# Layer 3 of a four-layer kernel: one pass over x3 in place of two

## Chip, cores and metric

The kernel runs on one core of a Trainium2 chip. The metric is the device time in microseconds (us) from start to end of one execution; three timed runs of the kernel before gave 3595.99 to 3599.18 us, median 3596.93 us. The profile is of one further execution.

A core has engines that run their own instruction streams in order and wait for each other through semaphores: PE (matrix products; PEld is its weight load), DVE (vector), ACT (activation functions), POOL (general), SP (here it only issues DMAs). DMAs move data between the memory of the chip (DRAM) and the 128 partitions of on-chip memory. PE writes its results to PSUM, a small memory from which DVE and ACT read.

## The reference, cut to what matters

The input is an image x of 256 x 256 positions with 128 channels. Four layers follow, each of the form x = x + layer(groupnorm(x)). The change concerns layer 3:

```python
    def _L3_conv_ref(x, w1, b1, w2, b2):
        H, W = (x.shape[1], x.shape[2])
        relu = jax.nn.relu
        def c1(t):
            return lax.conv_general_dilated(t, w1, (1, 1), 'SAME', dimension_numbers=DN) + b1
        w2c = w2[0, 4]
        def c2(t):
            return jnp.einsum('bhwc,cd->bhwd', t, w2c) + b2
        t = relu(c1(x))
        y = jnp.concatenate([x[:, :1], x[:, 1:] + t[:, :-1]], axis=1)
        u = relu(c1(y))
        z_main = u + jnp.roll(y, 1, axis=1)
        z = jnp.concatenate([z_main[:, :H - 2], u[:, H - 1:H] + y[:, H - 2:H - 1], y[:, H - 1:H]], axis=1)
        v = relu(c2(z))
        p = jnp.concatenate([z[:, :, :1], z[:, :, 1:] + v[:, :, :-1]], axis=2)
        r = relu(c2(p))
        q_main = r + jnp.roll(p, 1, axis=2)
        q = jnp.concatenate([q_main[:, :, :W - 2], r[:, :, W - 1:W] + p[:, :, W - 2:W - 1], p[:, :, W - 1:W]], axis=2)
        return q
```

`c1` is a convolution with nine taps along a row (w1 has the shape 1 x 9 x 128 x 1): it turns 128 channels into one, so t and u are single-channel images of 256 x 256. `c2` is a 128 x 128 product for each position. Since y is x plus t of the row above, and c1 is linear, c1(y) is c1(x) plus the nine taps of t of the row above, weighted with the sums of w1 over the channels. So the nine tap images of x are all that t and u need from x. z is x one row further up, plus a single-channel image e, which is made of u and of t two rows above.

## The kernel before

Layers 0 to 2 come first and leave their result in DRAM as `x3T` (128 channels x 65536 positions). Layer 3 then has three stages.

**p8** (L1116 to L1127), over 32 groups `s` of 2048 positions (eight rows): SP loads 1 MB of x3T into `p8_x` (L1119); four matmuls with `w1f`, the nine taps scaled by the groupnorm's factor, each write their 32 rows of one PSUM tile (L1122, `p_s` in the profile, which leaves out a stage's number in a name); ACT adds `s0` and writes `p_st` (L1126); POOL's queue stores it to the DRAM tensor `sD` (L147).

**img** (L1130 to L1189) makes e for the whole image at once: it loads all nine tap images into `St`, adds them with shifts along the row on DVE (L1153 to L1156), gets t on ACT, the nine taps of t by nine products and sums (L1163 to L1165), u, and e. Shifts by rows go from partition to partition, so t, the taps of t, u and e go through the DRAM tensor `imgD`: a store (`store`, L1136), then loads with the row shift in the address (`load_down`, L1141 and L1142; L1179 to L1187). e ends in `er` (L1206), one DMA for each of four positions groups.

**p9** (from L1199) is a second pass over x3 in 32 steps of eight rows (R = 8). Its order is written out by hand (`tc.manual_schedule()`), so each engine runs its part in the order of the text. In step s:

- `load9(s + 3)` loads nine rows of x3 (the row above is needed for z; L1217);
- ACT writes the first column of `pbs[s]` (L1289), `qs[s]` = x + constant (L1291), and `start_z(s + 1)` writes z without e (L1223);
- `p_half(s, 0)` and `(s, 1)`: two matmuls each into PSUM (`p_pm`, L1238), and a DVE instruction that makes p (L1246);
- `finish_z(s + 1)`: `broadcast_rows` spreads e over the partitions with PE (`p_eb`, L824), DVE adds it to z (L1232);
- `q_half(s - 1, ...)`: again two matmuls and DVE instructions (L1238, L1260, L1263) each, and one column on ACT (L1302);
- `residual(s)` on POOL (L1252 to L1254);
- `emit(s - 2)`: 16 transposes on PE (`p_pt`, L1275), two ACT copies (L1276), and one store of 1 MB by SP (L1277).

PSUM has two buffers for `p_pm` and two (tag "x") that `p_eb` and `p_pt` take in turn: the next user of such a buffer waits until DVE or ACT has read it.

Of the kernel before, what the change touches and what calls it, by code (L numbers as in the profile page):

```python
# [31 lines left out]
def kernel(ctx: ExitStack, tc: tile.TileContext, a: dict, out: bass.AP):  # L32
# [27 lines left out]
    sD = dram.tile([32, T], F32, name="sD")  # L60
    imgD = dram.tile([4, T], F32, name="imgD")
# [81 lines left out]
    b2 = column("L3_conv_b2")  # L143

# [52 lines left out]
    with tc.tile_pool(name="x0", bufs=1) as xres, tc.tile_pool(name="p0", bufs=3) as sb:  # L197
# [18 lines left out]
        with tc.tile_pool(name="f0", bufs=1) as fsb, tc.tile_pool(name="f0ps", bufs=1, space=PSUM) as ps:  # L216
# [29 lines left out]
            pb2 = ps.tile([P, 6], F32, name="f0_pb2")  # L246
# [4 lines left out]
            nc.vector.tensor_tensor(b2w, b2w, pb2, ALU.add)  # L251
            pt_ = ps.tile([P, NH], F32, name="f0_pt")
# [103 lines left out]
    with tc.tile_pool(name="p2c", bufs=1) as cs:  # L356
# [39 lines left out]
        with tc.tile_pool(name="p2", bufs=2) as sb, tc.tile_pool(name="p2e", bufs=6) as eb, tc.tile_pool(  # L396
# [159 lines left out]
            for j in range(2 * NG + 5):  # L556
# [5 lines left out]
                if not 0 <= out[0] < NG:  # L562
                    out = None
                if half == 0 and nxt:
                    tiles(nxt)
# [267 lines left out]
    rs2_pool = ctx.enter_context(tc.tile_pool(name="rs2", bufs=1))  # L833
# [262 lines left out]

    w1f = const.tile([P, 32], F32, name="w1f")
# [3 lines left out]
    kcol = const.tile([P, 3], F32, name="kcol")  # L1101
    with tc.tile_pool(name="f3", bufs=1) as sb, tc.tile_pool(name="f3ps", bufs=1, space=PSUM) as ps:
        pb = ps.tile([P, 1], F32, name="f3_s")
        for q in range(4):
            nc.tensor.matmul(pb[32 * q : 32 * q + 32, :], lhsT=w1f, rhs=m3, start=True, stop=True)
        nc.vector.tensor_scalar(s0, pb, -1.0, None, ALU.mult)
        nc.vector.scalar_tensor_tensor(k0, m3, -1.0, r3, ALU.mult, ALU.mult)

        pw = ps.tile([P, 1], F32, name="f3_w")
        nc.tensor.matmul(pw, lhsT=w2c, rhs=b2, start=True, stop=True)  # L1110
        nc.vector.tensor_scalar(kcol[:, 0:1], b2, -1.0, None, ALU.mult)
        nc.vector.scalar_tensor_tensor(kcol[:, 1:2], pw, -1.0, b2, ALU.mult, ALU.subtract)
        nc.vector.scalar_tensor_tensor(kcol[:, 2:3], b2, 2.0, pw, ALU.mult, ALU.add)

    with tc.tile_pool(name="p8", bufs=4) as sb, tc.tile_pool(name="p8ps", bufs=4, space=PSUM) as ps:
        for s in range(NSC):  # L1116
            ss = slice(s * SC, (s + 1) * SC)
            xt = sb.tile([P, SC], F32, name="p8_x", bufs=6)
            nc.sync.dma_start(xt, x3T[:, ss])  # L1119
            pp = ps.tile([P, CK], F32, name="p8_s")  # L1120
            for c in range(4):
                nc.tensor.matmul(  # L1122
                    pp[32 * c : 32 * c + 32, :], lhsT=w1f, rhs=xt[:, c * CK : (c + 1) * CK], start=True, stop=True
                )
            st = sb.tile([P, CK], F32, name="p8_st", bufs=8)
            nc.scalar.activation(st, pp, AF.Identity, bias=s0)  # L1126
            store_groups(nc.gpsimd, sD, s, st)  # L1127


    with tc.tile_pool(name="img", bufs=1) as sb, tc.tile_pool(name="imgps", bufs=1, space=PSUM) as ps:  # L1130

        def image(k):
            return imgD[k].rearrange("(h w) -> h w", w=N)

        def store(k, t):
            nc.sync.dma_start(image(k).rearrange("(t p) w -> p t w", p=P), t)  # L1136

        def load_down(t, k, n):

            nc.vector.memset(t[0:32, 0, :], 0.0)  # L1140
            nc.sync.dma_start(t[n:P, 0, :], image(k)[0 : P - n, :])  # L1141
            nc.sync.dma_start(t[:, 1, :], image(k)[P - n : N - n, :])  # L1142

        pw = ps.tile([P, TAPS], F32, name="pw")
        nc.tensor.matmul(pw, lhsT=ones, rhs=w1[:, :TAPS], start=True, stop=True)
        wsum = sb.tile([P, TAPS], F32, name="wsum")
        nc.vector.tensor_copy(wsum, pw)
        St = sb.tile([P, TAPS, 2, N], F32, name="St")
        nc.sync.dma_start(
            St.rearrange("p k t w -> p (k t) w"), sD[:TAPS, :].rearrange("k (t p w) -> p (k t) w", p=P, w=N)  # L1150
        )
        acc = sb.tile([P, 2, N], F32, name="acc")
        nc.vector.tensor_copy(acc, St[:, 4, :, :])  # L1153
        shifts = [(k, max(0, 4 - k), min(N, N + 4 - k)) for k in range(TAPS) if k != 4]
        for k, lo, hi in shifts:
            nc.vector.tensor_tensor(  # L1156
                acc[:, :, lo:hi], acc[:, :, lo:hi], St[:, k, :, lo + k - 4 : hi + k - 4], ALU.add
            )
        t_ = sb.tile([P, 2, N], F32, name="t_")
        nc.scalar.activation(t_, acc, AF.Relu, bias=b1)  # L1160
        store(0, t_)
        ct = sb.tile([P, 2, N], F32, name="ct")
        nc.vector.tensor_scalar(ct, t_, wsum[:, 4:5], None, ALU.mult)  # L1163
        for k, lo, hi in shifts:
            nc.vector.scalar_tensor_tensor(  # L1165
                ct[:, :, lo:hi], t_[:, :, lo + k - 4 : hi + k - 4], wsum[:, k : k + 1], ct[:, :, lo:hi],
                ALU.mult, ALU.add,
            )
        store(1, ct)
        cd = sb.tile([P, 2, N], F32, name="cd")  # L1170
        load_down(cd, 1, 1)
        nc.vector.tensor_tensor(acc, acc, cd, ALU.add)
        u_ = sb.tile([P, 2, N], F32, name="u_")
        nc.scalar.activation(u_, acc, AF.Relu, bias=b1)
        store(2, u_)

        eu = sb.tile([P, 2, N], F32, name="eu")
        nc.vector.memset(eu[96:P, 1, :], 0.0)
        nc.sync.dma_start(eu[:, 0, :], image(2)[0:P, :])  # L1179
        nc.sync.dma_start(eu[0 : P - 2, 1, :], image(2)[P : N - 2, :])  # L1180
        nc.sync.dma_start(eu[P - 2 : P - 1, 1, :], image(2)[N - 1 : N, :])
        et = sb.tile([P, 2, N], F32, name="et")
        nc.vector.memset(et[0:32, 0, :], 0.0)
        nc.sync.dma_start(et[0:1, 0, :], image(0)[N - 2 : N - 1, :])
        nc.sync.dma_start(et[2:P, 0, :], image(0)[0 : P - 2, :])
        nc.sync.dma_start(et[0 : P - 2, 1, :], image(0)[P - 2 : N - 4, :])
        nc.sync.dma_start(et[P - 2 : P, 1, :], image(0)[N - 3 : N - 1, :])  # L1187
        nc.vector.tensor_tensor(eu, eu, et, ALU.add)
        store(3, eu)  # L1189
# [8 lines left out]
    H = R // 2  # L1198
    with tc.tile_pool(name="p9", bufs=2) as sb, tc.tile_pool(name="p9psM", bufs=2, space=PSUM) as psM, tc.tile_pool(  # L1199
# [3 lines left out]
        xs, zs, pbs, qs = {}, {}, {}, {}  # L1203
        er = sb.tile([P, CK], F32, name="p9_e", bufs=1)
        for c in range(4):
            nc.sync.dma_start(er[32 * c : 32 * c + 32, :], imgD[3].rearrange("(s c t) -> c s t", c=4, t=CK)[c])  # L1206

        def load9(s):
            if s >= NR:
                return  # L1210
            h0 = s * R
# [7 lines left out]
        def start_z(s):  # L1219
# [4 lines left out]
            if n < R:  # L1224
                nc.scalar.activation(zs[s][:, n:R, :], xs[s][:, n + 1 :, :], AF.Identity, bias=k0, scale=r3)
# [55 lines left out]
        for s in range(3):  # L1281
            load9(s)
# [209 lines left out]
```

## Time and profile before

| what | us |
|---|---|
| median of three runs | 3596.93 |
| the profiled execution | 3590.95 |
| its span (first to last instruction) | 3589.0 |
| layers 0 to 2, and the groupnorm of layer 3, to the first load of x3T at | 3091.9 |
| p8 to its last stores, and St's load begins at | 3205.4 |
| img, to the first p_eb matmul at | 3251.0 |
| p9, to the end | 3589.0 |

The page gives for the whole span PE 87% busy, DVE 64%, ACT 54% and POOL 45%, and a mean granted PE clock of 0.93 of full speed. Those are means over all layers; the table above says where layer 3 lies, and the stage, not the mean, tells what bounds it. A row of the page's groups gives the line, the engine, the operation with output and inputs, how often it ran, its busy time and the mean time of one, and then the idle time before it with what ended that.

In p9's steady part a DMA pair looks like this on SP's queue: the output store is issued in 0.39 us (L1277, at 3377.26), and the load of x3 behind it takes 1.86 us to issue (L1217, at 3377.69), while such a load takes 0.42 us to issue where no store stands ahead (L1214).

### The profile page before, as it was taken

Reading aid. Unit: us, or ns where it says so; the run is one execution under the profiler, and the core shown is the slowest. Engines: PE = TensorE matmul, PEld = TensorE weight load, DVE = VectorE, ACT = ScalarE, POOL = GpSimd, SP = SyncE. Lnnn points to the kernel's source line nnn. Section 1 sums busy time; section 2 is a strip of 40 time slices with the busy share of each in tenths; the row PEclk is TensorE's granted clock in tenths of the full one; section 3 lists DMA queues with packets and bytes.
Section 4 is the critical chain, followed back from the end, with each engine's and each line's share of the span. In section 5 each row is a group of like instructions: output and inputs, shape, how many; then the busy total and the mean of one; then the engine's idle time right before and its main releaser. Section 6 shows DMA issues by size and latency. Waiting matters only on the chain. (4 is left out here: it accounts for less than half of the span.)

```text
span 3589.0 us, 52067 instructions
## 1 busy us (share of the span) xinstructions
PE 3130.1 (87%) x20266; PEld 1649.4 (46%) x20266; DVE 2280.2 (64%) x2522; ACT 1948.9 (54%) x2163; POOL 1631.0 (45%) x852
## 2 busy tenths in 40 slices
PE   4566999999999999955795999998998999636998
PEld 4413555555555555513332444446996333103544
DVE  4625888888888888831695454454555777215776
ACT  3564777777777777632343444443443566414665
POOL 3003777777777777612593000002554444313444
PEclk7887999999999999978897999999998999758999
DMA  9892333333333333278697778667997888675776
GB/s 329 317 344 91 102 119 113 108 114 119 114 110 111 119 117 111 92 296 314 215 329 316 260 259 304 230 245 281 352 351 282 339 336 335 267 284 172 227 226 187
DMA packets 276662, 801.88 MB, mean 223 GB/s; under 512 B 36639, under 2 KB 109612, under 8 KB 221884
## 3 DMA queue, kind: packets, MB, share of 16 engines
q1 hardware_dynamic: 256844, 780.41, 60.9%
q0 software_dynamic: 19568, 18.09, 1.7%
q8 instruction: 162, 2.65, 0.3%
q14 instruction: 88, 0.72, 0.1%
HBM read 504.22 MB, written 294.09 MB: 222 GB/s over the span
## 5 line engine op out<-in xcount | busy, mean ns | idle before, releaser
L468 DVE TENSOR_TENSOR p_e<-p_S,triT 128x1024 f32<-128x1024 f32 x512 | 609.4, 1212 | 144.5 <-PE p_S L458 144.5
L478 POOL TENSOR_TENSOR p_es<-p_e 128x1024 f32<-128x1024 f32 x256 | 603.0, 2366 | 127.5 <-issue 67.5
L476 ACT ACTIVATE p_e<-p_e,mbT 128x1024 f32<-128x1024 f32 x512 | 551.8, 1137 | 63.2 <-DVE p_e L468 61.4
L908 PE MATMUL p_pm<-p_zn,wf 128*128 128x512 f32 x1024 | 443.9, 595 | 15.8 <-DVE p_zn L901 15.8
L443 PE MATMUL p_mm<-p_xn,wf 128*128 128x512 f32 x768 | 409.0, 616 | 8.0 <-POOL p_xn L416 8.0
L416 POOL TENSOR_TENSOR p_xn<-p_xn,p_rs 128x1024 f32<-128x1024 f32 x64 | 153.6, 2400 | 446.4 <-DMA p_rs<-rsD 254.1
L908 PEld LDWEIGHTS p_pm<-p_zn,wf 128*128 128x128 f32 x1024 | 194.8, 191 | 265.1 <-issue 244.5
L458 PE MATMUL p_S<-p_q,p_k 32*128 32x256 f32 x4096 | 295.3, 400 | 5.0 <-DVE p_e L468 5.0
L458 PEld LDWEIGHTS p_S<-p_q,p_k 32*128 32x128 f32 x4096 | 185.8, 184 | 161.5 <-PE p_mm L434 91.7
L1450 PE MATMUL tp_z<-p_B,tp_at 128*128 128x256 f32 x1024 | 250.6, 388 | 0.8 <-DMA p_B<-bD 0.5
L491 PE MATMUL p_o<-p_e,p_v 128*32 128x256 f32 x4096 | 249.2, 384 | 0.0
L1252 POOL TENSOR_TENSOR p_q<-p_q,p_pb 128x2024 f32<-128x2024 f32 x32 | 144.1, 4502 | 220.8 <-DVE p_pb L1246 220.8
L1079 POOL TENSOR_TENSOR p_x<-p_x,p_g 128x2048 f32<-128x2048 f32 x32 | 145.4, 4544 | 182.6 <-DVE p_g L1076 182.6
L1000 POOL TENSOR_TENSOR p_k<-p_k,p_sq 128x512 f32<-128x512 f32 x128 | 162.9, 1273 | 135.8 <-ACT p_sq L998 135.8
L962 POOL DMA_DIRECT2D rs__17975<-rs2D x4 | 2.1, 519 | 466.7 <-DMA rs2D<-p_vc 466.7
L1450 PEld LDWEIGHTS tp_z<-p_B,tp_at 128*128 128x128 f32 x1024 | 185.1, 191 | 23.2 <-DVE tp_at L1441 1.5
L443 PEld LDWEIGHTS p_mm<-p_xn,wf 128*128 128x128 f32 x768 | 126.7, 191 | 113.3 <-issue 90.2
L491 PEld LDWEIGHTS p_o<-p_e,p_v 128*32 128x32 f32 x4096 | 120.5, 110 | 110.0 <-ACT p_g L449 41.5
L999 DVE TENSOR_TENSOR p_k<-tp_z,p_k 128x512 f32<-128x512 f32 x128 | 88.5, 692 | 127.0 <-ACT p_sq L998 127.0
L996 ACT COPY p_K<-tp_z 128x512 f32<-128x512 f32 x128 | 75.1, 586 | 165.4 <-PE tp_z L1450 165.4
L434 PEld LDWEIGHTS p_mm<-wf,p_xn 128*128 128x128 f32 x1024 | 135.5, 193 | 62.9 <-issue 61.9
L939 DVE SCALAR_TENSOR_TENSOR p_b<-p_pm,b2w,p_b 128x1024 f32<-128x1024 f32 x64 | 82.2, 1284 | 125.4 <-PE p_pm L908 111.0
(335 smaller groups left out, 5870.3 us busy)
## 6 DMA issues: line engine op xcount, KB each, us to landing
p_x<-x2T SPq DMA_DIRECT2D x64, 1024.0 KB
p_x<-x1T SPq DMA_DIRECT2D x48, 1024.0 KB
p_x<-x3T SPq DMA_DIRECT2D x31, 1152.0 KB
p_x<-x3T SPq DMA_DIRECT2D x33, 1024.0 KB
p_x<-in_x_dram SPq DMA_DIRECT2D x32, 1024.0 KB
p_x<-xT SPq DMA_DIRECT2D x64, 512.0 KB
p_rs<-rsD SPq DMA_DIRECT2D x64, 512.0 KB
p_rb<-rzD SPq DMA_DIRECT2D x256, 128.0 KB
```

The lines of the kernel that those rows point to most:

```text
L416: nc.gpsimd.tensor_tensor(xn, xn, t["rs"], ALU.mult)
L443: nc.tensor.matmul(pm, lhsT=w, rhs=t["xn"][:, cs_], start=True, stop=True)
L458: nc.tensor.matmul(Ss[h // 2][:, h % 2, u, :], lhsT=t["k"][hp, r * N + u * P : r * N + (u + 1) * P], rhs=t["q"][hp, r * N : (r + 1) * N], ...
L468: nc.vector.tensor_tensor(e[:, :, 2 * p : 2 * p + 2, :].rearrange("p u h n -> p h u n"), Ss[p], triT[:, 2 * p : 2 * p + 2, :, :], ALU.add,)
L476: nc.scalar.activation(e[:, u, :, :], e[:, u, :, :], AF.Exp, bias=mbT[:, u, i : i + 1])
L478: nc.gpsimd.tensor_tensor(es, e[:, 0, :, :], e[:, 1, :, :], ALU.add)
L491: nc.tensor.matmul(t["o"][hp, r % 2, :], lhsT=t["v"][:, r * 2 + u, hp], rhs=e[:, u, h, :], start=(u == 0), stop=(u == 1),)
L908: nc.tensor.matmul(pm[:, c, :], lhsT=wf2[:, i, :], rhs=zns[s][:, k * CK : (k + 1) * CK], start=True, stop=True)
L1000: nc.gpsimd.tensor_tensor(k2, k2, sq, ALU.add)
L1079: nc.gpsimd.tensor_tensor(xs[s], xs[s], gt, ALU.add)
L1252: nc.gpsimd.tensor_tensor(q[:, :, 1 : N - 2], q[:, :, 1 : N - 2], pb[:, :, 0 : N - 3], ALU.add)
L1450: nc.tensor.matmul(pz[:, t, :], lhsT=at[:, u, t * P : (t + 1) * P], rhs=Bc[:, u, :], start=(u == 0), stop=(u == 1))
```

## The change

p8 and img are gone, and p9 does their work in passing. Only one pass over x3 is left.

- `load9` loads eight rows, not nine, into nine buffers (four before), eight steps ahead (three before). The row above comes from the step before's tile, so `start_z` takes two ACT instructions.
- `taps(x, h0, n)` does p8's work for the row group six steps ahead: four matmuls into a PSUM tile `p9_pp` of the two buffers with tag "x" that p_eb and p_pt use too, one ACT instruction to `p9_st`, and four stores by SP (nine tap rows by two image rows each) to `sD`, whose rows are now padded to 264 with zeros or large negative numbers; three small DMAs in layer 0 (at j == 20) fill the padding.
- `load_block(b)` handles 16 image rows (two steps). Partition 16 q + i holds the row i of the block and the columns 32 q onward. The shift of each tap along the row, and the row shift, lie in the DRAM addresses (`sD_shift` has a tap pitch longer by one). Sixteen DMAs of 16 partitions, nine taps and 40 or 32 columns.
- `sum_taps(b)`: one DVE reduction over the nine taps and two short instructions give t. `keep_t(b)` stores t to `tD` and reads it back shifted by a row. `image_u(b)`: one product with nine overlapping windows of t, one reduction and two short instructions. `image_e(b)`: one sum, a store to `eD`, and four small DMAs into one of two `er` tiles.
- In the loop, an even step s sums block b = s//2 + 2 behind p_half and makes u at its end; the odd step behind it makes e and then loads block b + 1.
- The sums of the taps' weights and the constants `kcol` are worked out in layer 0.

```diff
-    with tc.tile_pool(name="p8", bufs=4) as sb, tc.tile_pool(name="p8ps", bufs=4, space=PSUM) as ps:
-        for s in range(NSC):
...
-    with tc.tile_pool(name="img", bufs=1) as sb, tc.tile_pool(name="imgps", bufs=1, space=PSUM) as ps:
...
         def load9(s):
...
+            if s < NR:
+                xs[s] = sb.tile([P, R, N], F32, name="p9_x", bufs=9)
+                nc.sync.dma_start(xs[s], x3r[:, s * R : (s + 1) * R, :])
+
+        def taps(x, h0, n):
+
+            pp = psX.tile([P, 2, CK], F32, name="p9_pp", tag="x")
+            for c in range(n):
+                nc.tensor.matmul(
+                    pp[32 * c : 32 * c + 32, 0, :], lhsT=w1f, rhs=x[:, 2 * c : 2 * c + 2, :], start=True, stop=True
+                )
+            st = sb.tile([P, 2, N], F32, name="p9_st", bufs=3)
+            nc.scalar.activation(
+                st[0 : 32 * n].rearrange("p h w -> p (h w)"), pp[0 : 32 * n, 0, :], AF.Identity, bias=s0[0 : 32 * n]
+            )
+            for c in range(n):
+                at = 8 + (h0 + 2 * c + 1) * NP
+                nc.sync.dma_start(
+                    sD_tap[:, at : at + 2 * NP].rearrange("k (h w) -> k h w", w=NP)[:, :, 0:N],
+                    st[32 * c : 32 * c + TAPS],
+                )
+
+        def load_taps(St, b, up, lo, hi, width, at):
+
+            for q in range(8):
+                first = (b * BR + lo - up + 1) * NP + 32 * q + (40 - width) // 2
+                src = sD_shift[:, first : first + (hi - lo) * NP].rearrange("k (h w) -> h k w", w=NP)
+                nc.sync.dma_start(St[BR * q + lo : BR * q + hi, :, at : at + width], src[:, :, 0:width])
+
+        def load_block(b):
+            St = sb.tile([P, TAPS, 72], F32, name="p9_S")
+            load_taps(St, b, 1, 0, BR, 40, 32)
+            load_taps(St, b, 0, 0, BR, 32, 0)
+            blocks[b] = dict(St=St)
...
+        def sum_taps(b):
+
+            k = blocks[b]
+            k["acc"] = sb.tile([P, 72], F32, name="p9_acc")
+            nc.vector.tensor_reduce(k["acc"], k["St"].rearrange("p k w -> p w k"), AX.X, ALU.add)
+            k["t"] = sb.tile([P, 40], F32, name="p9_t")
+            nc.vector.scalar_tensor_tensor(k["t"], k["acc"][:, 32:72], b1, inside, ALU.add, ALU.mult)
+            nc.vector.tensor_scalar(k["t"], k["t"], 0.0, None, ALU.max)
+
+        def keep_t(b):
+            k = blocks[b]
+            nc.sync.dma_start(t_rows(b * BR - 1), k["t"][:, 4:36])
+            k["t2"] = sb.tile([P, 32], F32, name="p9_t2")
+            nc.sync.dma_start(k["t2"], t_rows(b * BR - 2))
...
+        def image_e(b):
+
+            k = blocks.pop(b)
+            e = sb.tile([P, 32], F32, name="p9_e")
+            nc.vector.tensor_tensor(e, k["u"], k["t2"], ALU.add)
...
+                nc.sync.dma_start(e_rows[:, b * BR : (b + 1) * BR, :], e)
...
+            for c in range(4):
+                nc.sync.dma_start(
+                    ers[b % 2][32 * c : 32 * c + 2, :],
+                    eD.rearrange("o (s c t) -> c (o s) t", c=4, t=CK)[c, 2 * b : 2 * b + 2, :],
+                )
...
         for s in range(NR + 2):
-            load9(s + 3)
+            load9(s + 8)
+            b = s // 2 + 2
...
                 p_half(s, 0)
                 p_half(s, 1)
                 del xs[s]
+            if s % 2 == 0 and b < NB:
+                sum_taps(b)
+                keep_t(b)
             if s + 1 < NR:
                 finish_z(s + 1)
...
             if s < NR:
                 residual(s)
+            if s + LEAD < NR:
+                taps(xs[s + LEAD], (s + LEAD) * R, 4)
+            if s % 2 == 0 and b < NB:
+                image_u(b)
+            if s % 2 == 1 and b < NB:
+                image_e(b)
+                if b + 1 < NB:
+                    load_block(b + 1)
             if s > 1:
                 emit(s - 2)
```

Ahead of the loop the new kernel makes the first blocks in a row: it loads the last two rows (for t of row 254, which the first row of e needs) and groups 0 and 1, makes their taps, loads and sums block 0, makes t, u and e of it; then the same with groups 2 and 3 for block 1, and groups 4 and 5 for block 2, whose loads are issued ahead of step 0.

## The prediction

> **What bounds the kernel now.** I read the table of stages first, then the chain of waits through layer 3, then the groups of the last stage by shape, then SP's own queue in order of time. Everything before 3091.9 us belongs to the layers that the change leaves alone but for a few tiny instructions, so only the last 497 us count.
>
> Stages of layer 3 (columns named in the first line):
>
> ```profile
> core 0: us, PE busy (x) PEld busy (x) DVE busy (x) ACT busy (x) POOL busy (x), PEclk, DMA share, GB/s
> 3091.90:3140.00 48.10, 27.06 (x134) 4.01 (x138) 0.59 (x5) 9.62 (x14) 9.59 (x14) 0.61 0.99 403
> 3140.00:3205.00 65.00, 28.72 (x138) 3.97 (x130) 0.00 (x0) 12.26 (x18) 12.48 (x19) 0.61 0.95 348
> 3205.00:3250.00 45.00, 0.00 (x0) 0.00 (x0) 14.74 (x24) 1.44 (x2) 0.00 (x0) 0.50 0.29 95
> 3250.00:3290.00 40.00, 31.22 (x95) 13.63 (x96) 23.22 (x23) 18.69 (x16) 14.57 (x9) 0.83 0.51 187
> 3290.00:3560.00 270.00, 270.00 (x1094) 135.29 (x1093) 206.41 (x220) 170.22 (x166) 132.36 (x82) 1.00 0.69 222
> ```
>
> The first 113 us (p8, first pass over x3) are DMA at 0.95 to 0.99; the next 45 us (img) are a serial image chain with an idle PE; then PE is busy every moment. In the chain of waits the steady step repeats every 9.88 us (p_pm 3.44, p_eb 1.07, p_pm 3.63, p_pt 1.75).
>
> Steady stage, groups by shape (busy us, mean ns):
>
> ```profile
> L1246 DVE SCALAR_TENSOR_TENSOR p_pb<-p_pm,kcol,p_z 128x1020 f32<-128x1020 f32 x54 | 69.1, 1280 | 51.2 <-PE p_pm L1238 51.2
> L1260 DVE SCALAR_TENSOR_TENSOR p_q<-p_pm,kcol,p_q 128x1016 f32<-128x1016 f32 x52 | 65.9, 1268 | 0.0
> L1232 DVE TENSOR_TENSOR p_z<-p_eb,p_z 128x1024 f32<-128x1024 f32 x54 | 63.6, 1219 | 11.5 <-ACT p_z L1223 11.5
> L1291 ACT ACTIVATE p_q<-p_x,kcol 128x2048 f32<-128x2048 f32 x27 | 54.0, 1999 | 0.0
> ```
>
> SP and DVE in order of time (start, length), the price list of small DMAs:
>
> ```profile
> 3224.12 0.24 SPq L1184 DMA_DIRECT2D et<-imgD  x1
> 3224.41 0.34 SPq L1185 DMA_DIRECT2D et<-imgD  x1
> ...
> 3243.81 0.26 SPq L1181 DMA_DIRECT2D eu<-imgD  x1
> 3245.75 0.69 DVE L1188 TENSOR_TENSOR eu<-eu,et 128x512 f32<-128x512 f32 x1 [5.76 <-DMA eu<-imgD]
> 3246.47 0.38 SPq L1136 DMA_DIRECT2D imgD<-eu  x1
> 3248.63 1.69 SPq L1206 DMA_DIRECT2D p_e<-imgD  x4
> ```
>
> From these: one-row DMAs follow each other every 0.29 us, 16-engine ones every 0.42 (1.69/4); a store that is read back costs 2.16 us from its issue to the next issue (3246.47 to 3248.63); a load reaches DVE 1.94 us after its issue (3243.81 to 3245.75).
>
> PE after a pause, another stage:
>
> ```profile
> 1640.94 1.92 PE L676 MATMUL p<-x,v 128*32 128x512 f32 x16
> ...
> 1653.47 5.25 PE L676 MATMUL p<-p_x,v 128*32 128x512 f32 x32 [5.86 <-DMA p_x<-x1T]
> ```
>
> After 5.86 us of idleness 32 matmuls take 5.25 us where 2 x 1.92 is usual: 1.4 us lost to the clock.
>
> **What the Trainium skill says.** "DMA: Bandwidth & Descriptors", section "Two DMAs through the same engine are not ordered": a DMA that reads what another wrote must wait for its completion semaphore. The trace agrees, at 2.16 us a hop. Same page, "Why a DMA increments its semaphore by 16 and not by 1": the engines used are the largest number up to 16 that divides the slowest dimension on both sides. The trace agrees: cd<-imgD with 127 rows takes 8.09 us in the chain of waits. So block loads (16 rows) use 16 engines, tap stores (9 rows) nine. "TensorE: Matmul & The Clock Gate", "Part 1: The HAM clock gate": an idle window of about 3.4 us halves the clock, a busy one restores it. The 5.25 us above agree.
>
> **The change part by part.**
>
> *Removed:* p8 and img. The first p_eb starts at 3251.0 now.
>
> *Added to PE:* a step's taps, four matmuls into 32-row slices; p8 shows 1.06 us at full clock for the same eight instructions. 9.88 + 1.07 = 10.95 us a step, 22 us per block of two. ACT gets a 0.69 us st and a second small p_z (some 0.25), DVE some 3 us per block; neither fills 22 us.
>
> *Start-up.* The x3 loads start at the same 3091.9. SP's queue is followed with the prices above, with nothing beside it (all other engines wait for it):
> - two rows and groups 0 and 1 land by about 3100 (p8's first group came 5.0 us after its issue, the next 2.4 later); taps, ACT, nine stores: 3104.0. The read-back waits for landing: 3105.7. Eight one-row loads for t of row 254 take 2.4, sixteen loads for block 0 take 6.7: 3114.9.
> - x groups 2 and 3, then eight stores of that t. The program takes eight DMA semaphores in turn, so each DMA waits for the landing of the one eight before it; the last of these waits for x 3: 3122.4. Then t of block 0 out (2.2), back (2.2), e and out (2.4), and four er (1.2): 3130.4. The first p_eb can follow near 3131.
> - block 1: eight tap stores 2.6, landing 1.7, sixteen loads 6.7: 3141.4. Three x loads go ahead of its t, so t lands behind 3 MB, at about 3151.5; back, e out and landed, er: 3157.4.
> - block 2: 2.6 + 1.7 + 6.7, and 1.7 to land: its sum starts on DVE near 3171. That sum stands ahead of finish_z(1) on DVE, so the steps can't run away before it.
>
> *The loop.* In SP's order load_block(b+1) comes after the tap stores of step s+1, the store of e(b), and er(b), which waits for e; DVE needs it in step s+2 behind p_half. Sixteen DMAs and two hops sit on that path. From the start of sum_taps(b), at 0:
> - DVE: sum 1.3 (72 x 9 elements by the 0.69 us of 512, an estimate, and two short ones), finish_z 2.4, two q_half 2.7, image_u 1.3: 7.8.
> - Step s+1: p_half's two results to 10.7; finish_z(s+2) waits for ACT's p_z (pt copies 1.9, pb 0.3, q 1.9, z 2.2 in a row) until 11.2, done 13.6; q_half frees PE, taps, st: 15.7.
> - SP: four tap stores 0.33 each: 17.0; e stored and landed 2.2: 19.2; four er 0.29 each: 20.4; sixteen loads 0.42 each: 27.1; landing 1.7: 28.8.
>
> So a block takes 28.7 us, not 22. In it PE idles over 6 us before the next taps (DVE holds the PSUM of p_eb), and then starts at half clock, which I take as plus 1.5 (from the 1.4 above): 30.2 us. The wait for the block has finish_z, q_half and image_u behind it on DVE, PE's taps and transposes behind these, then ACT's copies and the output stores. SP's own wait for t's landing holds the tap stores, but these are not late by it.
>
> Unknown costs. A block load's issue: 0.29 (one-row row) to 0.60 us (twice the one-row, for three-dimensional addresses); I take 0.42, the nearest row of 16 engines. Landing 1.3 to 2.2; taken 1.7. The strided reduction 0.85 to 1.4, taken 0.85. Clock 0 to 3 us per block, taken 1.5. The weights' new instructions, and three fills on SP in layer 0: nothing to 5 us; taken as nothing, since layer 0 loads two groups ahead; uncovered, the 2322 pieces of the first fill are the 5.
>
> *Sum.* Blocks 2 to 15 are summed in the loop: 13 periods. 3171 + 13 x 30.2 (393) + 69 from the sum of block 15 to the end (step 27's p_half starts some 4 us after it; now it runs from 3524.4 to 3589, 64.6 us) = 3633. Against the span of 3589.0 this is +44; the profiled run lies 1.95 us outside its span at 3590.95, the median at 3596.93, so 3641.
>
> **Rivals.**
> 1. *The chain per block sets the pace* (above, slower): for it, the 13.1 us on SP between st (15.7) and the sum (28.8) stand against the 5.4 us of work that PE has left there (p_pt 1.75, p_half 3.63). It decides from a period of 26.8 us on: (3589 - 3171 - 69) / 13.
> 2. *PE stays the bound, SP keeps up* (faster): 3171 + 13 x 22 + 69 = 3526, 3534 as a median. It needs SP's 13.1 us cut to about 5.4, or a part of them off the path in a way that my reading of the two queues misses. For it, DMA is only 0.69 busy in the steady stage, so the bytes are no obstacle; against it, no row shows an issue below 0.2 us or a landing below 1.3.
> 3. *About level*: issues at 0.33 us and landings at 1.3 give 26.9 us with a warm PE: 3171 - 6 + 350 + 69 = 3584, 3592.
> 4. *SP's issues are dearer* (0.60): 33.2 us with clock loss; start-up 8 us later: 3179 + 432 + 69 = 3680, 3688; with 3 us of clock per block 3708.
>
> **How the numbers follow.** Rival 1: 0.60, its own range 3612 to 3680. Rival 2: 0.14. Rival 3: 0.11, spread over both signs. Rival 4: 0.15. A difference below 0.2% (7 us) can't be told from none. Faster: rival 2 and 0.06 of rival 3, 0.20; same: the rest of rival 3, 0.05; slower: 1 and 4, 0.75. The range, 3565 to 3720, takes in 1, 3 and 4 and leaves out rival 2 and a little beyond 4's dearest end.
>
> **What would show it.** Right: after 3170 us, 14 waits of DVE at the reduction, released by the p9_S loads, 6 to 9 us each; blocks every 30 us; SP issuing sixteen loads in 6.7 us; PE near 0.75 busy with a clock below 1.00. Start-up right if the first p9_eb comes near 3131. Wrong: a reduction that doesn't wait and steps of 11 us (rival 2), or loads that take 0.3 or 0.6 us to issue.

## The result and the profile after

| | before | after |
|---|---|---|
| median, us (four runs each) | 3596.46 | 3660.57 |
| lowest to highest, us | 3593.34 to 3599.18 | 3659.47 to 3667.12 |
| span of the profiled execution, us | 3589.0 | 3658.7 |
| mean granted PE clock | 0.930 | 0.927 |
| first load of x3 in layer 3, us | 3091.9 | 3097.6 |

After to before is 1.0182, 95% interval 1.0165 to 1.0200: the change makes the kernel some 64 us slower. The forecast of 3641 us (3565 to 3720) has the sign and the mechanism, and is 20 us short.

The stages of the kernel after, in the same columns as those of before:

```profile
core 0: us, PE busy (x) PEld busy (x) DVE busy (x) ACT busy (x) POOL busy (x), PEclk, DMA share, GB/s
3091.90:3180.00 88.10, 23.11 (x86) 6.15 (x86) 16.10 (x39) 15.14 (x19) 6.17 (x7) 0.54 0.36 112
3180.00:3300.00 120.00, 92.68 (x352) 41.08 (x352) 69.43 (x92) 53.68 (x60) 36.76 (x22) 0.86 0.46 139
3300.00:3560.00 260.00, 192.93 (x778) 88.42 (x776) 148.78 (x198) 114.98 (x128) 79.69 (x51) 0.88 0.51 151
```

Read the row from 3300 on first: PE is busy for 192.93 of 260 us, at a clock of 0.88, where before it was busy for all of it at 1.00; DMA is busy for half. No engine is the bound. So the next view is who waits for whom, between 3170 and 3600 us (total, times, longest; the last line is of SP's own queue):

```profile
PEld p_pp L1176 <- DVE p_z L1272: 128.0, 25, 17.4
DVE p_acc L1211 <- DMA p_S<-sD: 117.0, 14, 13.4
PE p_pp L1176 <- DVE p_z L1272: 108.2, 13, 16.6
SPq L1185 <- ACT p_st L1180: 90.4, 15, 8.7
```

PE's taps (L1176) wait for DVE's finish_z, and DVE waits in 14 places at the reduction (L1211) for the block loads, 8.4 us each. SP's queue is not simply full: ahead of the tap stores it waits itself, for an st that ACT hasn't written yet. The third question is what SP does meanwhile. One period, from one sum to the next, in order of time (start, length; SPq is SP's queue):

```profile
3398.54 1.30 DVE L1211 TENSOR_REDUCE p_acc<-p_S 128x72 f32<-128x648 f32 x1 [7.71 <-DMA p_S<-sD]
...
3401.54 1.94 PE L1176 MATMUL p_pp<-p_x,w1f 128*32 128x512 f32 x8 [7.32 <-DVE p_z L1272]
...
3413.91 1.06 PE L1176 MATMUL p_pp<-p_x,w1f 128*32 128x512 f32 x8
...
3415.05 0.69 ACT L1180 ACTIVATE p_st<-p_pp,s 128x512 f32<-128x512 f32 x1 [3.56 <-PE p_pp L1176]
3415.76 1.36 SPq L1185 DMA_DIRECT2D sD<-p_st  x4
...
3417.55 0.59 SPq L1240 DMA_DIRECT2D eD<-p_e  x1
3419.54 1.21 SPq L1248 DMA_DIRECT2D p_er<-eD  x4
3420.86 7.43 SPq L1195 DMA_DIRECT2D p_S<-sD  x16
...
3429.93 1.30 DVE L1211 TENSOR_REDUCE p_acc<-p_S 128x72 f32<-128x648 f32 x1 [8.29 <-DMA p_S<-sD]
```

The period is 31.39 us, and its last 14 lie in SP's queue, one DMA or landing behind the other: four tap stores, the store of e, its landing, four er loads, sixteen block loads, landing. The same eight tap matmuls take 1.94 us right after a pause, at a granted clock of 0.50 (3401.5 to 3403.5), and 1.06 us a step later, at 1.00 (3413.9 to 3415): that is what the clock costs there. All the sums of the loop, 3179.85 for block 2 to 3588.31 for block 15, are 31.4 us apart on average: 17.7 us from the start of a sum to the end of the odd step's st, and 13.7 from there to the next sum. The experiments are read by these two parts.

### The profile page after: what moved, and what is told of

The parts are those of the page before. It is cut to its first block, busy times and chain, and to the rows that moved or that the text cites. A ratio compares the mean times of both kernels' runs of the same rounds, so it can differ in the third digit from the quotient of the medians.

```text
span 3658.7 us, 52810 instructions
## 1 busy us (share of the span) xinstructions
PE 3145.3 (86%) x20268; PEld 1662.8 (45%) x20268; DVE 2316.5 (63%) x2634; ACT 1958.3 (54%) x2194; POOL 1610.1 (44%) x824
## 4 chain that ended last, share of the span: by engine, by line
PE 40%; DMA 7%; SPq 4%; DVE 2%; issue 2%; POOL 1%; ACT 1%; DVEq 0%; ACTq 0%; POOLq 0%
PE p_pm L943 12%; PE tp_z L1551 6%; PE p_pm L1089 6%; PE p_pm L1278 4%; SPq L1195 3%; PE p_pg L808 2%; DMA abD<-p_ab 2%; PE tp_a L1540 2%; PE p_pt L1315 2%; PE p_st L900 1%; DMA x2T<-p_x 1%; PE p_pp L1176 1%; PE p_rz L858 1%; PE p_rk L858 1%; PE p_pz L816 1%
## 5 line engine op out<-in xcount | busy, mean ns | idle before, releaser
L943 PE MATMUL p_pm<-p_zn,wf 128*128 128x512 f32 x1024 | 443.6, 595 | 15.7 <-DVE p_zn L936 15.7
L1176 PE MATMUL p_pp<-p_x,w1f 128*32 128x512 f32 x256 | 50.6, 875 | 146.5 <-DVE p_z L1272 108.2
L1180 ACT ACTIVATE p_st<-p_pp,s 128x512 f32<-128x512 f32 (+1 forms) x33 | 22.7, 688 | 270.6 <-PE p_pp L1176 227.1
```

The costliest lines, as they stand in the source:

```text
L943: nc.tensor.matmul(pm[:, c, :], lhsT=wf2[:, i, :], rhs=zns[s][:, k * CK : (k + 1) * CK], start=True, stop=True)
```

## The experiments

Theory 1 is the forecast's: SP's chain between the last taps of a block and its sum sets the period. Against it stood a lockstep of PE, DVE and ACT with a cold clock (each waits for the others' last results, so that a step takes its time whatever SP does), and the bytes or pieces of the small loads instead of their issue. Ratios are to the kernel before, run beside each; the period is the mean distance of the sums within one profile, up to block 15, from block 2 on for the changed kernel and runs 1, 3 and 7, and from block 3 on for the others, where the distance from block 2 to block 3 still belongs to the start-up. (From block 2 on, these would differ by 0.6 us at most.)

| run | ratio to before (95%) | period, us |
|---|---|---|
| the changed kernel | 1.0182 (1.0165 to 1.0200) | 31.4 |
| 1 block loads ahead of e | 1.0135 (1.0115 to 1.0155) | 29.8 |
| 2 sum one step later | 1.0140 (1.0120 to 1.0160) | 30.3 |
| 3 half the block loads on ACT | 1.0113 (1.0092 to 1.0134) | 29.8 |
| 4 before, with the additions to layer 0 | 1.0019 (1.0010 to 1.0028) | |
| 5 new order on SP, e at the head of a step | 1.0231 (1.0198 to 1.0263) | 32.9 |
| 6 as 5, sum behind p_half | 1.0308 (1.0267 to 1.0349) | 35.5 |
| 7 block loads issued twice as often | 1.0523 (1.0488 to 1.0558) | 39.1 |
| 8 t read between the loads, e later | 1.0126 (1.0106 to 1.0147) | 29.8 |
| 9 as 8, taps seven groups ahead | 0.9972 (0.9960 to 0.9984) | 25.5 |
| 10 the changed kernel, taps seven ahead | 1.0052 (1.0034 to 1.0070) | 28.3 |
| 11 as 9, large transfers on ACT's queue | 0.9939 (0.9919 to 0.9958) | 24.6 |
| 12 as 11, e behind q_half | 1.0058 (1.0036 to 1.0081) | 27.7 |

**Run 7: is it the issue, or the bytes?**

```diff
-                nc.sync.dma_start(St[BR * q + lo : BR * q + hi, :, at : at + width], src[:, :, 0:width])
+                for k0_, k1_ in ((0, 5), (5, TAPS)) if hi - lo == BR else ((0, TAPS),):
+                    nc.sync.dma_start(
+                        St[BR * q + lo : BR * q + hi, k0_:k1_, at : at + width], src[:, k0_:k1_, 0:width]
+                    )
```

> The changed kernel with every block load split into two (taps 0 to 4 and 5 to 8): the same bytes and the same pieces of 128 and 160 bytes, 32 issues instead of 16. Theory 1 with the issue as the price: 16 x 0.46 = 7.4 us more in each of 13 periods and about 20 in the start-up's three blocks: 3660 + 96 + 20 = 3776, with a period of 38.8. If the time of a load is that of its pieces or bytes in the DMA engines, an issue of half the pieces takes half as long: 3655 to 3670. Lockstep as the bound: 3655 to 3670 too.

Measured: 3784.25 us, a period of 39.1. SP's queue in this run:

```profile
3419.03 1.36 SPq L1185 DMA_DIRECT2D sD<-p_st  x4
3420.49 0.60 SPq L1243 DMA_DIRECT2D eD<-p_e  x1
3422.36 1.20 SPq L1251 DMA_DIRECT2D p_er<-eD  x4
3423.66 14.85 SPq L1196 DMA_DIRECT2D p_S<-sD  x32
```

32 issues take 14.85 us, 0.464 each, exactly what sixteen took each (7.43 / 16), though each carries half the data. The whole execution moves the same 760.4 MB in both kernels. So a block load's price is its issue on SP, and the period grew by 7.7 us for 7.4 us more of it. Nearly all of it is in the part from st to the sum, 21.1 us instead of 13.7; the other part is 18.0 instead of 17.7. The issue as the price and its place in the chain are shown, and the lockstep falls as the bound.

**Run 1: e off the path.**

```diff
             if s % 2 == 1 and b < NB:
-                image_e(b)
                 if b + 1 < NB:
                     load_block(b + 1)
+                image_e(b)
```

> In the odd steps the sixteen loads of the next block are issued ahead of image_e, so the e store, its landing and the four er loads (about 3.8 us in the trace of the changed kernel: 3417.12 to 3420.86) no longer stand between the tap stores and the block loads. Theory 1 (SP's chain of tap stores, e, er, loads and landing sets the period): period 31.4 - 3.8 = 27.6 us, 13 periods save 49, so some 3611 us. Rival A (the lockstep of PE, DVE and ACT with a cold PE clock sets the period, and the wait at the reduction is only where the slack gathers): no change, 3655 to 3665. Rival B (the whole is bound by SP's work, whatever its order): no change in the period, since SP issues the same DMAs; 3655 to 3665, but with SP busy or waiting all the time.

Measured: 3641.25 us, 19 less than the changed kernel instead of 49. SP's queue shows why:

```profile
3406.89 1.36 SPq L1185 DMA_DIRECT2D sD<-p_st  x4
3409.52 7.42 SPq L1195 DMA_DIRECT2D p_S<-sD  x16
3417.05 0.60 SPq L1240 DMA_DIRECT2D eD<-p_e  x1
```

The loads now wait 1.27 us (3408.25 to 3409.52) for the tap stores to land. In the changed kernel this landing was hidden under the store of e and its reading back. So taking away 3.7 us uncovers 1.3. In the mean, the part from st to the sum fell by 1.8 us, to 11.9, and the period by 1.6; where the last half microsecond went was not followed.

**Run 3: two queues.**

```diff
-            load_taps(St, b, 0, 0, BR, 32, 0)
+            load_taps(St, b, 0, 0, BR, 32, 0, nc.scalar)
```

> The eight loads of the unshifted half of each block (width 32) are issued by ACT instead of SP; bytes and descriptors are the same. Theory 1 with the issues as its largest part (16 x 0.46 us): SP's stretch is shorter by 8 x 0.46 = 3.7 us, ACT issues its eight while SP waits for e; period 27.7, 13 periods and the start-up (three blocks) save about 48 + 11, so 3600 to 3615 us. If it is not the issue but the DMA engines that take the time (small pieces of 128 bytes), the loads land no sooner: 3650 to 3665. Rival A (lockstep with ACT in it): ACT has 3.7 us more in each block, so 3660 to 3710.

Measured: 3635.62 us; the period fell by 1.7 us, not by 3.7. The part from st to the sum did fall as forecast, from 13.7 us to 10.2, but the other part grew from 17.7 to 19.5. ACT stood 78.8 us in 12 waits ahead of its copies, at its own block loads, which wait for the tap stores. These waits lie ahead of the sum, which still waited for its loads; but ACT's q, late by them, now released GpSimd's residual (the bracket of the second line), and the sum, which came earlier, ran into it (DVE and POOL of this run in order of time):

```profile
3414.03 1.33 DVE L1211 TENSOR_REDUCE p_acc<-p_S 128x72 f32<-128x648 f32 x1 [4.29 <-DMA p_S<-sD]
3414.33 4.49 POOL L1292 TENSOR_TENSOR p_q<-p_q,p_pb 128x2024 f32<-128x2024 f32 x1 [10.58 <-ACT p_q L1381]
3415.39 3.48 DVE L1213 SCALAR_TENSOR_TENSOR p_t<-p_acc,b,p_in 128x40 f32<-128x40 f32 x1
```

The second operation of the sum, 0.26 us in the changed kernel, takes 3.48 and ends at 3418.87, when POOL's (3418.82) does; finish_z and the taps stand behind it.

**Run 2: the sum one step later.**

```diff
-            if s % 2 == 0 and b < NB:
+            if s % 2 == 1 and b < NB:
                 sum_taps(b)
                 keep_t(b)
...
+            if s % 2 == 0 and 2 < b <= NB:
+                image_e(b - 1)
```

image_u moves with the sum, and the block loads stay at the end of the odd step.

> sum_taps, keep_t and image_u of a block move from the even step to the odd step after it, image_e to the even step after that; the block loads stay where they are. The block load then has one whole step more to arrive. Theory 1: the wait at the reduction goes; what is late next is PE (two steps of 10.95 us = 22 us a block) or SP's queue (its DMAs and its waits for t and e, some 24 us a block by the trace). The steps may also begin before the sum of block 2. About 3160 + 15 x 23.5 + 28 = 3541 in the span, 3525 to 3580 as a time, so faster than both kernels. Rival A (PE, DVE and ACT in lockstep with a cold clock set the period): 3640 to 3665. Rival B (SP's work is the bound, with about 31 us a block): 3640 to 3665.

Measured: 3640.72 us, near rivals A and B. The waits at the block loads are gone from the loop, and yet the period is 30.3 us. SP's queue says which rival, from the store of t on:

```profile
3393.33 0.59 SPq L1218 DMA_DIRECT2D tD<-p_t  x1
3398.81 0.61 SPq L1220 DMA_DIRECT2D p_t<-tD  x1
3400.79 1.38 SPq L1185 DMA_DIRECT2D sD<-p_st  x4
3403.34 7.42 SPq L1195 DMA_DIRECT2D p_S<-sD  x16
...
3414.99 0.60 SPq L1240 DMA_DIRECT2D eD<-p_e  x1
3419.26 1.21 SPq L1248 DMA_DIRECT2D p_er<-eD  x4
```

SP waits in order: 4.9 us for t to land (3393.92 to 3398.81), 3.7 for e (3415.59 to 3419.26), both behind 2 MB of output and x3 issued just ahead. PE then waits for er (64.3 us in 12 waits at p_eb). With these waits SP's round, all that it issues and waits for in a block, comes near 30 us, and it waits for ACT's st no more than 21.1 us in 12: rival B in the main. And DVE's short operation takes 3.42 us here too.

**Runs 5 and 6: the price of GpSimd, and a mistake of mine.** Both sum in the odd step, store t between tap stores and block loads, read it back behind the loads, put e at the head of the even step, and load er behind that step's tap stores. They differ in one place: run 5 sums behind q_half, run 6 behind p_half. From run 5 to run 6:

```diff
+            if s % 2 == 1 and b < NB:
+                sum_taps(b)
             if s + 1 < NR:
                 finish_z(s + 1)
...
             if s % 2 == 1 and b < NB:
-                sum_taps(b)
                 keep_t(b)
                 image_u(b)
                 if b + 1 < NB:
                     load_block(b + 1)
                 read_t(b)
```

> Every read-back on SP gets something to cover its landing. Odd step: tap stores, sum_taps and keep_t behind q_half (when GpSimd's long sum is over), the store of t between the tap stores and the block loads, the read of t behind the block loads. Even step: e at its head and its store ahead of the tap stores, the four er loads behind them. Theory 1 in its wider form (SP's queue, issues and waits for landings in a row, sets the period whatever the order of the other engines): the waits for t (5.4 us a block in the run with the later sum), for e (3.7) and the 3.4 us of the sum's second operation go; 30.3 - 9 = 21 is below what PE needs, so PE is the bound at 22 us a block: 3160 + 15 x 22.5 + 28 = 3525 in the span, 3520 to 3560 as a time, and PE's clock goes back to near 1.00 between 3300 and 3560. Rival A (the back-pressure of the 1 MB stores and loads makes SP's issues themselves the bound, some 25 us a block): 3565 to 3590. Rival B (the lockstep of PE, DVE and ACT sets 30 us): 3625 to 3650.

> As the run with the new SP order, but the sum stands behind p_half on DVE, when GpSimd's 4.5 us sum of the same step runs. If DVE's second operation of the sum (both operands in SBUF) is held until GpSimd's instruction ends, it takes 3.4 us instead of 0.26 here, with finish_z and q_half behind it: 13 or 14 blocks x 3.2 = some 42 us more than the run with the sum behind q_half, or a part of that if DVE has slack. If the 3.4 us had another cause (the place of the block load in SBUF, or the load still landing), it takes 0.26 in both, and both times agree within 10 us.

Measured: 3678.65 (run 5) and 3706.61 us (run 6). Against each other they settle the side question, with periods of 32.9 and 35.5. The first line is of run 5, the others of run 6:

```profile
3390.75 0.26 DVE L1213 SCALAR_TENSOR_TENSOR p_t<-p_acc,b,p_in 128x40 f32<-128x40 f32 x1
...
3396.38 4.47 POOL L1296 TENSOR_TENSOR p_q<-p_q,p_pb 128x2024 f32<-128x2024 f32 x1 [8.04 <-DVE p_pb L1290]
3397.49 3.41 DVE L1213 SCALAR_TENSOR_TENSOR p_t<-p_acc,b,p_in 128x40 f32<-128x40 f32 x1
```

The Trainium skill, "GPSIMD Engine Reference", section "Key points", says that GpSimd shares its SBUF interfaces with VectorE, and that DVE instructions with two SBUF inputs contend; here both inputs (p_acc, p_in) lie in SBUF, and the trace agrees. finish_z, which reads PSUM and SBUF, lost nothing beside POOL (2.36 us at 3421.12 in run 9, while POOL's sum runs from 3420.87 to 3425.38).

Both are slower than the changed kernel, against the expectation, because of my placing of e (run 5):

```profile
3399.49 0.63 SPq L1222 DMA_DIRECT2D p_t<-tD  x1
...
3401.68 0.19 DVE L1239 TENSOR_TENSOR p_e<-p_u,p_t 128x32 f32<-128x32 f32 x1 [8.97 <-DMA p_t<-tD]
...
3403.12 5.20 PE L1282 MATMUL p_pm<-p_pb,w2c 128*128 128x512 f32 x8 [8.57 <-DVE p_pb L1290]
```

SP read t behind all sixteen loads; DVE stood 9 us for it ahead of p_half, and PE with it, which then ran at a mean clock of 0.71 (5.20 us for what takes 3.70).

**Runs 8, 9 and 10: how much lead the chain needs.** Run 8, from run 5:

```diff
-            if s % 2 == 0 and 2 < b <= NB:
-                image_e(b - 1)
...
                 finish_z(s + 1)
+            if s % 2 == 0 and 2 < b <= NB:
+                image_e(b - 1)
...
             load_taps(St, b, 1, 0, BR, 40, 32)
+            if between is not None:
+                read_t(between)
             load_taps(St, b, 0, 0, BR, 32, 0)
```

Run 9 is run 8 with one row group more of lead, so that each of its parts moves one step forward; run 10 gives this lead to the changed kernel alone (the taps of group 6 go into the start-up in both):

```diff
-    LEAD = 6
+    LEAD = 7
...
             if s % 2 == 0 and b < NB:
                 image_u(b)
+                if b + 1 < NB:
+                    load_block(b + 1)
             if s % 2 == 1 and b < NB:
                 image_e(b)
-                if b + 1 < NB:
-                    load_block(b + 1)
```

> As the run with the new SP order (whose steps stood still because e, put at the head of DVE's even step, waited 9 us for the t2 read that SP issued behind all sixteen loads), with two places changed: SP reads t2 between the first eight and the last eight block loads, and DVE computes e behind finish_z of the even step. Theory 1 (the chain through SP sets the period): t2 lands some 6 us after the odd step's taps, e is wanted 7 us after them, so no engine waits for SP any more; SP has about 20 us of DMAs a block by the trace, PE 22, so PE bounds: 3160 + 15 x 22.5 + 28 = 3525 in the span, 3520 to 3565 as a time. Rival A (SP's 20 us and its waits don't fit into the step's order, and one of them still holds DVE): 3565 to 3630. Rival B (lockstep of PE, DVE and ACT with a cold clock at 30 us a block, whatever SP does): 3630 to 3680.

> Taps seven row groups ahead instead of six, so that a block's taps, loads, sum and e all come one step earlier against their use, with the order of the last run otherwise (t2 read between the halves of the block loads, sum behind q_half, e behind finish_z). In the last run the er loads came 5 to 6 us late for PE each block, because the store of e landed behind 2 MB of x and output in the same queue; with a step of 11 us more they are in time. Theory 1 (what sets the period is the chain through SP's queue): nothing waits for SP any more, PE bounds at 22 us a block, clock near 1.00 from 3300 to 3560: 3160 + 15 x 22.5 + 28 = 3525 in the span, 3520 to 3565 as a time, below both kernels. Rival B (lockstep of PE, DVE and ACT with a cold clock at 30 us): 3620 to 3660. Rival A (the sum of SP's issues and waits is itself about 28 us a block): 3590 to 3620.

> The changed kernel with taps seven row groups ahead and the block loads in the even step in which those taps are made, nothing else: sum_taps, keep_t, image_u and image_e stay where they are, so SP still waits in order for t and for e to land. Theory 1: the chain from the taps to the sum has 11 us more than the 31 it needs in 22, so no single wait at the sum is left; but SP's own round (some 20 us of issues, 4.4 to 5.5 us of waiting for t, 2 to 3.7 for e) is 27 to 30 us: 3570 to 3635, SP never idle except in these waits. If latency alone was the matter: PE-bound, 3520 to 3565. If lockstep sets 30 us: 3640 to 3665.

Measured: 3636.02, 3583.45 and 3610.80 us. Run 8 has two changes, which are not told apart; in it the wait went on to the last link, er: PE waits for it 57.1 us in 13. One more step of lead gives run 9 a period of 25.5 and a time below before (0.9972, 0.9960 to 0.9984), but not the 22 of theory 1: SP still waits 37.0 us in 13 for the tap stores and 40.3 in 14 for e. Run 10 shows that lead alone does not do it: it needs 28.3 us, and SP waits 52.4 us for t and 45.3 for e in 12 blocks each; its issues and these waits fill its queue, as theory 1 said of that run.

**Runs 11 and 12: the large transfers in another queue.**

```diff
-            load9(s + 8)
...
                 if s + 1 < NR:
                     start_z(s + 1)
+                load9(s + 8, nc.scalar)
...
-            nc.sync.dma_start(
+            nc.scalar.dma_start(
                 out_tok[s * SC : (s + 1) * SC, :].rearrange("(k p) d -> p k d", p=P), ot
             )
```

> As the last run with taps seven ahead, but the two large transfers of a step (1 MB of x3 in, 1 MB out) are issued by ACT in its own queue, the output right behind ACT's copies, x behind its p_z. In the last run SP still waited 3 to 4 us a block each for the tap stores and for e, and DVE 4 us for t, all small transfers that land behind these 2 MB. Theory 1 with the shared queue as the reason for the long landings: these waits fall to the 1.3 to 2 us that a small store takes alone, the 1.4 us that SP's x loads took behind an output store go from SP, SP's round is some 17 us, and PE bounds: 22 to 23 us a block, 3515 to 3555 as a time. If small transfers are slow because the DMA engines are shared by all queues: waits and time as in the last run, 3570 to 3595. If ACT can't take the issues (0.4 and up to 1.4 us a step, beside some 7 us of work): 3580 to 3620.

Run 11: 3572.22 us, the best of all; 0.9939 of before, and the period 24.6. Its steady stage, in the columns of before:

```profile
3300.00:3540.00 240.00, 224.12 (x945) 104.35 (x944) 182.84 (x237) 146.49 (x160) 99.26 (x63) 0.99 0.56 164
```

PE is back at 0.93 busy and a clock of 0.99. SP's wait for e fell from 40.3 us (14 waits, run 9) to 3.1 (5), that for the tap stores from 37.0 (13) to 3.8 (12): the long landings were those of the shared queue. But other waits came up, of SP for the landing of x3 loads (33.8 us in 11) and of block loads (37.2 in 18), though SP's DMAs there use none of their data, and DVE still waited 33.4 us in 12 for t. So the gain is 1.0 us a block, not the 3 expected. Part of the profiled execution's 3561.3 us of span is chance: its layer 3 began at 3085.3.

Run 12 moves e on DVE:

```diff
-            if s % 2 == 1 and b < NB:
-                image_e(b)
             if 0 < s <= NR:
                 q_half(s - 1, 0)
                 q_half(s - 1, 1)
...
                 del pbs[s - 1], zs[s - 1]
+            if s % 2 == 1 and b < NB:
+                image_e(b)
```

> As the last run (bulk on ACT's queue), but DVE computes e behind q_half of the odd step instead of ahead of it. There DVE stood 2.5 to 3.6 us a block (33.4 us in 12) before e for the t2 read, with q_half and so PE's next p_pm behind it. Theory 1 (each wait of the SP chain that has a step's work queued behind it is paid in full, one without is free): period 24.5 - 2 to 2.5 = 22 to 22.5 us, PE's own 22; 12 to 14 blocks save 25 to 30 us: 3540 to 3555. If PE is held as much by something else (ACT's issues, p_z 0.4 us later for each step) and this wait was beside it: 3565 to 3580. If e then comes too late for its er loads: 3580 or more, with PE waiting for them at p_eb.

It came out slower than run 11 by 1.2%: 3612.41 us. From SP's list of waits in run 12 (total, times, longest):

```profile
SPq L1185 <- DMA out_dram<-p_o: 75.3, 12, 6.6
```

The tap stores (L1185), which need nothing but st, now wait 6.3 us each for an output store to land. The trace's semaphore numbers say why. The program's DMAs in both queues take the same eight semaphores in turn, and each waits until the earlier user of its semaphore has landed. In all 12 waits that user was an output store of ACT's queue: the tap store issued at 3383.99 waits for semaphore 115, which the output store of 3379.19 had taken and which was complete at 3383.97. So a second queue did not set SP free of the large transfers; run 11's waits for x3 loads are of this kind too, and the move of e changed which DMAs share a semaphore. t came late in its turn (82.5 us in 12 at e). Whether DVE's wait was worth its 2 us stays open.

**Run 4: the additions to layer 0.** The kernel before with the weights' small sums, results unused, and the three fills, in DRAM of their own:

```diff
+            pb2 = ps.tile([P, TAPS + 1], F32, name="f0_ps", tag="f0_pb2")
+            nc.tensor.matmul(pb2[:, :TAPS], lhsT=ones, rhs=w1[:, :TAPS], start=True, stop=True)
+            nc.vector.tensor_copy(wsum0, pb2[:, :TAPS])
...
+                if j == 20:
+                    nc.sync.dma_start(
+                        sD_tap.rearrange("k (h w) -> k h w", w=NP)[:, :, 0:8],
+                        fill[:, 0:1, :].to_broadcast([TAPS, N + 2, 8]),
+                    )
...
```

> The kernel before, with only what the change adds outside layer 3: the tiny weight sums (wsum and kcol, into tiles of their own that nobody reads) and the three fills in layer 0 (into DRAM of their own). If these are the cause of the 5.7 us by which the changed kernel's layer 3 starts later, 3601 to 3604 against 3596.5. If the tiny products alone count (1.5 us on the path), 3597.5 to 3599. If the 5.7 us come from elsewhere (where the buffers lie, or chance from one execution to the next): 3594 to 3598.

Measured: 1.0019 (1.0010 to 1.0028), in 22 runs against 27: 3.6 to 10 us dearer than before. The median, 3597.40, lies 4.3 above. So the additions are not free, and their size fits the 5.7 us of later start. Which of them costs it stays open. The products stand on the path (gn_pm, the next matmul there, starts at 175.14 instead of 170.47 us, 1.5 us of it behind f_ps), and the rest is not told apart from chance: the profiles of the changed kernel's relatives, alike up to layer 3, show its first row group loaded anywhere from 3085.3 to 3103.6 us. Against that spread, the 5.7 us of one pair of profiles say little by themselves; run 4's interval is what counts.

## Why the prediction was right, and where it was short

**The chain, its order, its place: right.** Fourteen waits at the reduction, predicted at 6 to 9 us each, came to 117.0 us, 8.4 each (the longest 13.4). PE's share, predicted near 0.75, is 0.74. The odd step's st ended 17.7 us after the start of the sum in the mean (17.2 in the period shown), where the text had 15.7 and 1.5 for the clock. In that period the taps and transposes right after the pause took 1.35 us more than a step later, so the clock's term was about right.

**The period, 30.2 predicted, 31.4 measured: mis-sized terms.** In the mean, the part up to st is 0.5 us longer than the 17.2 predicted, and the part from st to the sum 0.6 longer than the 13.1 (13.7; the rest is rounding, as the working carries its 28.8 on as 28.7). By the period shown above, whose second part is longer than most (14.2 us):

| from the end of st | predicted | measured |
|---|---|---|
| tap stores | 1.3 | 1.4 |
| e stored and landed | 2.2 | 2.4 |
| four er | 1.2 | 1.3 |
| sixteen block loads | 6.7 | 7.4 |
| landing | 1.7 | 1.6 |

The largest is the issue of the block loads: 0.464 us each, not the 0.42 of the nearest row, 0.7 us in every period; run 7 confirms it. The value lies in the bounds given (0.29 to 0.60). Over 13 periods the 1.2 us are 15.6. The reduction, taken at 0.85, takes 1.30 us: about as much as the part up to st is longer in the mean. In the period shown other terms made up for it, which is luck.

**Layer 0, costed at nothing within a bound of 5 us: wrong.** Layer 3 starts 5.7 us later in the profile; run 4 puts the additions at 3.6 to 10 us of time. The cover that the text named, loads two groups ahead, does not hide the products, which stand in the groupnorm's path.

**Start-up: 79.1 us predicted from the first load to the sum of block 2, 82.3 measured.** The first p_eb came at 3139.9, not near 3131: 42.3 us behind the first load, where the text had 39.1, so the loss lies ahead of it. The largest term: the 24 loads ahead of the first sums took 13.46 us, and sixteen of them take 7.42 (block 1), so the eight one-row loads for row 254 took 0.75 us each, not 0.29, 3.7 us in all. The loads of three blocks at 7.4 instead of 6.7 add 2.2, and other terms came out some 2.7 shorter.

**The tail: 69 predicted, 70.4 measured.** In sum: 44 forecast, and 5.7 + 3.1 + 15.6 + 1.4 on top make 69.8; the span grew by 69.7. Of these, the 5.7 rests on one pair of profiles.

**The rivals.** That SP keeps up (3534) and the level case fell with the 13.1 us from st to the sum, measured at 13.7 in the mean. Dearer issues (0.60) came true in a small part. What the text missed about its own remedy is that "a part of them off the path" does not bring 22 us a block: run 1 uncovered a landing, run 2 SP's own round, run 8 the er loads, and the best of all still needs 24.6.

## What to carry to other kernels

When a pass is saved by moving its work into another, count the DMA issues and the stores that are read back on the queue that takes them: here they held a block at 31.4 us where PE's own work is 22 by the forecast's estimate, and with 82 us of start-up that outweighed the 159 us of the two stages saved. Such a chain needs a lead that exceeds its latency, and no run here made it quite free. A row group more of lead gained more (1.3%, run 10) than any reordering on the path, and small stores that are read back were better off in another queue than the megabytes (run 11), as far as the two queues don't share semaphores (run 12). After a wait is removed, look for the next in order: runs 1, 3 and 11 gained less than half of what the removed part had cost.

## What the runs showed of the hardware

- The issue of these small DMAs on SP went with their form, not with their bytes: 0.464 us for 16 rows of nine pieces, and the same with five or four pieces (run 7); 0.34 for a tap store (nine rows of two pieces); 0.30 for two rows of er; 0.75 for one row of nine pieces (worked out above).
- DVE's two-SBUF-input operation of 40 elements a row took 3.4 us beside GpSimd's 4.5 us sum, and 0.26 without it (runs 6 and 5); the reduction ahead of it, with one input, took 1.33 us beside that sum (run 3) and 1.30 to 1.34 without (the changed kernel, run 5).
- A strided sum of nine (648 elements a row, the nine 288 bytes apart) took 1.30 us, that of 288 neighbouring elements 0.45: 2.0 against 1.6 ns an element.
- A small store issued behind 2 MB in its own queue was waited for 3.7 to 4.9 us (runs 2 and 10); with the 2 MB in ACT's queue SP hardly waited for such stores. The Trainium skill, "DMA: Bandwidth & Descriptors", section "Queues, rings and completion order", says that each DMA engine consumes one ring in order and takes turns between queues; runs 9 and 11 agree.
